# A state-space, attention and feed-forward kernel on one core: the skip term D u moved from TensorE to VectorE in PSUM, and other weights for the steps between the feed-forward's products

## The chip, the cores and the metric

The kernel runs on one core of one Trainium2 chip. The metric is the device time of one execution in microseconds. Five engines work side by side, each through its own queue in order: PE (TensorE, matmuls), DVE (VectorE), ACT (ScalarE), POOL (GpSimd) and SP (SyncE, which issues most of the transfers). Matmul results are written to PSUM, of which the kernel uses eight banks of 128 partitions by 512 fp32 values.

## The reference, cut to what matters

The input is 8 images of 384 channels and 32 x 32 pixels. Two layers follow each other; everything is fp32.

```python
# layer 0, per image, in both directions over L = 1024 pixels
u, z   = split(in_proj(rmsnorm(x)));  u = silu(causal_conv4(u))
dt, B, C = split(x_proj(u));  delta = softplus(dt_proj(dt) + bias)
h[l] = exp(delta * A) * h[l-1] + delta * u * B[l]        # 16 states per channel
y    = sum_n h[l, n] * C[l, n] + u * D_param             # u * D_param is the skip term
g    = out_proj(y * silu(z))                             # forward and backward are added
x    = x + res_scale * (scale_mod * g + sigmoid(dwconv3x3(xn)) * xn)
# layer 1
t = t + attention(layernorm(t))                          # 6 heads, causal over 1024 tokens
h = quant(W1b @ layernorm(t) + b1)                       # scale from max |h| of the whole image
t = t + quant(W2b @ gelu(h) + b2)                        # feed-forward, images 0 to 4 alone here
```

The scale of quant needs the maximum over all of h, so the Gelu and the second product can start only when the first product is complete. Work for other images can be placed in between.

## The kernel before, in words

**Tiles.** Channels lie on the 128 partitions, in three chunks c of 128. The 1024 tokens are cut in two halves h of 512, one PSUM bank each. The images are handled in the order 0, 1, 2, 3, 5, 6, 4, 7.

**Stages.** `before_scan(b)` normalises an image, projects it, does the short convolution, the gates (`gates`, 16 tap multiply-adds of the local convolution on DVE, Silu and Tanh on ACT), the x-projection (`project`) and the step sizes (`delta`). It writes to DRAM what the scan reads. The scan works through 96 units of two states per image. A unit has a multiply on POOL (`s_first`, L588), two exponentials on ACT (L601), two scans on DVE (L606), a second multiply on POOL (L612), and eight transposes with accumulation on PE (`s_sum`, L620), which sum the states in the bank `y`. `attention(b)` does the output projection, the attention and, for images 0 to 4, collects the steps of `feed_forward(b)`.

**The gate.** When a chunk's half is complete in both directions, `s_gate` puts it together, 48 times in all. It loads the half of u (`us`, the sum over both directions) and of silu(z) (`sz`) from DRAM, into one buffer each. It takes a bank of the tag `pt`, which has two. On PE it multiplies u by a diagonal matrix of D (`diagd`, built at the start, L183; the product is L656, two matmul instructions in the trace, as for every fp32 product here) and adds the transposed sums of the scan onto it (L661). DVE multiplies the bank by `sz` (L670) and SP writes the result out. The profile's names are `yb` for the bank, `ush` for the loaded u and `zh` for the loaded silu(z).

**The feed-forward.** It has 24 first-product steps (`hp`, L995), then the scale of h (`quant_scale`: a maximum on DVE, one transposition on PE named `row_h`, L963, and four small DVE operations), then the Gelu step (four ACT instructions over 128 x 3072, L1018, and four DVE minima, L1021, both raised in priority by 60 instructions), then six second-product steps (`yp`, L1039), a second scale (`row_y`) and three output steps. The weights of both products are loaded by SP as they are needed, from a pool of ten buffers (`mid`) that `before_scan` also uses.

**The order.** Each stage emits its work as steps, pairs of a function and an estimated length in us (2.5 if none is given). `spread_over` merges two lists so that both advance at the same share of their own total: a step's place is its middle divided by its list's total. The steps of a feed-forward are merged in this way with those of a later image's `before_scan`, for the first four images of the order (the later images are 5, 6, 4 and 7). The lengths in the merged list are multiplied by `JOINT` = 0.6. The feed-forward of image 4 has nothing left to be merged with. All lists of attention and feed-forward are joined to `rest`, and the scan units are placed evenly between due times that are sums of the lengths in `rest`. The resulting order is an order of priority: the framework's scheduler then makes each engine's queue from it, and may put an instruction that is ready before one that is not. Instructions in `pin` keep their written order.

The lines that do the merging:

```python
        if fed and later:
            fed = spread_over(fed, steps_of(before_scan, later.pop(0), ("pt", "pt", "av")))
            fed = [(f, JOINT * us) for f, us in fed]
        rest += fed
```

Of the kernel before, what the change touches and what calls it, by code (L numbers as in the profile page):

```python
# [12 lines left out]
ALU = mybir.AluOpType  # L13
# [4 lines left out]
P = 128  # L18
B, C, H, W = 8, 384, 32, 32
L = H * W  # L20
NC = C // P
# [18 lines left out]
DW = BC0 + 2 * NS  # L40
PARTS = ((0, 0), (0, 1), (1, 1), (1, 0))
JOINT = 0.6
SET = 8
HURRY = 400
AHEAD = 2
# [4 lines left out]
V_NORM, V_CW, V_CB, V_DTB, V_D, V_DW, V_DWB, V_BP, V_B2, V_ALOG = 0, 1, 5, 6, 7, 8, 17, 18, 19, 20  # L50
# [4 lines left out]
def kernel(  # L55
# [16 lines left out]
    nc = tc.nc  # L72
# [11 lines left out]
    def ctile(name, shape, dt=F32):  # L84
        return const.tile(shape, dt, name=name, tag=name)
# [44 lines left out]
    vec = ctile("vec", [P, NC, NV])  # L130
# [8 lines left out]
    for d in range(2):  # L139
        nc.scalar.dma_start(out=wdt[d * DW : d * DW + RANK, :], in_=w_dt)  # L140
        nc.scalar.dma_start(
            out=wdt[d * DW + RANK : d * DW + RANK + 1, :],
# [13 lines left out]
    ident = ctile("ident", [P, P])  # L156
# [21 lines left out]
    amat = ctile("amat", [P, NC, NS])  # L178
    nc.scalar.activation(amat, vec[:, :, V_ALOG : V_ALOG + NS], AF.Exp)
    nc.vector.tensor_scalar(amat, amat, -1.0, None, ALU.mult)  # L180
    diagd = ctile("diagd", [P, NC, P])
    for c in range(NC):
        nc.vector.tensor_scalar(diagd[:, c, :], ident, vec[:, c, V_D : V_D + 1], None, ALU.mult)  # L183
    rssm = ctile("rssm", [P, 1])
    nc.vector.tensor_tensor(rssm, sc[:, 0:1], sc[:, 1:2], ALU.mult)
    rsh = ctile("rsh", [P, 1])
# [357 lines left out]
    class Unit:  # L544
        def __init__(self, b, part, c, n):
            self.b, self.c, self.part, self.n = b, c, part, n
            self.d, self.h = PARTS[part]
            self.name = f"{b}_{c}_{part}_{n}"
            self.asks = c == (0 if n % (2 * SET) < SET else NC - 1)

# [3 lines left out]
        for part in range(len(PARTS))  # L554
        for k in range(NS // SET)
        for c in (range(NC) if k % 2 == 0 else reversed(range(NC)))
        for n in range(k * SET, (k + 1) * SET, 2)
    ]
# [84 lines left out]
    def s_gate(u):  # L643

        if not u.last:
            return
        b, c, h = u.b, u.c, u.h
        yts = sst.pop(("yt", b, c, h))
        both = []
        for what in ("us", "z"):  # L650
            t = sp.tile([P, HB], F32, name=f"{what}h_{u.name}", tag=what, bufs=1)
            load(t, spilled[b, what, c][:, half(h)])
            both.append(t)
        us, sz = both
        tp = bank(f"yb_{u.name}", "pt")
        nc.tensor.matmul(  # L656
            out=tp, lhsT=diagd[:, c, :], rhs=us, start=True, stop=False, skip_group_check=True
        )
        for yt in yts:
            for i in range(QT):  # L660
                nc.tensor.matmul(  # L661
                    out=tp[:, chunk(i)],
                    lhsT=yt[:, i, :],
                    rhs=ident,
                    is_transpose=True,
                    start=False,
                    stop=(yt is yts[-1] and i == QT - 1),
                    skip_group_check=True,
                )
        nc.vector.tensor_tensor(sz, sz, tp, ALU.mult)  # L670
        t = dram.tile([P, HB], F32, name=f"sgy_{u.name}", tag=f"sp_gy_{c}_{h}")
        nc.sync.dma_start(out=t, in_=sz)
        spilled[b, "gy", c, h] = t
# [296 lines left out]
    def feed_forward(b, t, emit):  # L970
        st = {}

        @emit
        def _():
            st["xn"] = t()
            st["mxh"] = small.tile([P, NF], F32, name=f"mxh_{b}", tag="mxh", bufs=1)
            st["mxy"] = small.tile([P, NC], F32, name=f"mxy_{b}", tag="mxy", bufs=1)

        layernorm(t, f"nf_{b}", emit)
        for m in range(NF):  # L980
            for h in range(NH):

                @emit.of(3.1)
                def _(m=m, h=h):
                    if m % NC == 0 and h == 0:
                        st["h", m // NC] = btile(f"h{m // NC}_{b}")
                    if m % 2 == 0 and h == 0:
                        st["w1"] = mtile(f"w1_{b}_{m}").rearrange("p (c e) -> p c e", c=4)
                        load(
                            st["w1"][:, :NC, :],  # L990
                            w1s[:, m * P : (m + 2) * P].rearrange("(c p) e -> p c e", p=P),
                        )
                    hp = bank(f"hp_{b}_{m}_{h}", "s")
                    for c in range(NC):
                        nc.tensor.matmul(  # L995
                            out=hp,
                            lhsT=st["w1"][:, c, chunk(m % 2)],
                            rhs=st["xn"][:, c, half(h)],
                            start=(c == 0),
                            stop=(c == NC - 1),  # L1000
                        )
                    hm = st["h", m // NC][:, m % NC, :]
                    nc.scalar.activation(hm[:, half(h)], hp, AF.Identity, bias=b1t[:, m : m + 1])
                    if h == NH - 1:
                        nc.vector.tensor_reduce(
                            st["mxh"][:, m : m + 1], hm, AX.X, ALU.max, apply_absolute_value=True
                        )

        @emit.of(3.0)
        def _():  # L1010
            st["s1"] = quant_scale(st["mxh"], f"h_{b}")


        @emit.of(3.0)
        def _():
            with tc.high_priority(offset=60):
                for q in range(NF // NC):
                    pin(nc.scalar.activation(st["h", q], st["h", q], AF.Gelu, scale=st["s1"]))  # L1018
                pin(nc.scalar.preload_act_table_set(LOG_EXP))
                for q in range(NF // NC):  # L1020
                    nc.vector.tensor_scalar(st["h", q], st["h", q], QCLIP, None, ALU.min)  # L1021

        for m in range(NC):
            for h in range(NH):

                @emit.of(10.7)
                def _(m=m, h=h):
                    if m == 0 and h == 0:
                        st["y"] = btile(f"yf_{b}")
                    if h == 0:  # L1030
                        for k in range(0, NF, 6):
                            w = mtile(f"w2_{b}_{m}_{k}", 6 * P).rearrange("p (k e) -> p k e", k=6)
                            load(
                                w, w2s[k * P : (k + 6) * P, chunk(m)].rearrange("(k p) e -> p k e", p=P)
                            )
                            st["w2", k // 6] = w
                    yp = bank(f"yp_{b}_{m}_{h}", "s")
                    for k in range(NF):
                        nc.tensor.matmul(  # L1039
                            out=yp,  # L1040
                            lhsT=st["w2", k // 6][:, k % 6, :],
                            rhs=st["h", k // NC][:, k % NC, half(h)],
                            start=(k == 0),
                            stop=(k == NF - 1),
                        )
                    ym = st["y"][:, m, :]
                    nc.scalar.activation(
                        ym[:, half(h)], yp, AF.Identity, bias=vec[:, m, V_B2 : V_B2 + 1]
                    )
                    if h == NH - 1:  # L1050
                        nc.vector.tensor_reduce(
                            st["mxy"][:, m : m + 1], ym, AX.X, ALU.max, apply_absolute_value=True
                        )

        @emit.of(3.0)
        def _():
            st["s2"] = quant_scale(st["mxy"], f"y_{b}")

        for m in range(NC):

            @emit
            def _(m=m):
                to = mtile(f"t3_{b}_{m}")
                load(to, spilled[b, "t2", m])
                for h in range(NH):
                    ym = bank(f"yq_{b}_{m}_{h}", "s")
                    nc.vector.tensor_scalar(
                        ym, st["y"][:, m, half(h)], st["s2"], QCLIP, ALU.mult, ALU.min
                    )
                    th = to[:, half(h)]  # L1070
                    nc.vector.scalar_tensor_tensor(th, ym, -QCLIP, th, ALU.max, ALU.add)
                nc.sync.dma_start(out=out[b, chunk(m), :], in_=to)


    class Steps(list):
# [4 lines left out]

        def of(self, us):
            return lambda f: self(f, us)

    def spread_over(*lists):

# [64 lines left out]
    for i, b in enumerate(ORDER):  # L1150
        if i > 0:
            due.append((sum(us for _, us in rest), i * per))
        fed = Steps()
        rest += steps_of(attention, b, fed) if i < B - 1 else []
        if fed and later:
            fed = spread_over(fed, steps_of(before_scan, later.pop(0), ("pt", "pt", "av")))
            fed = [(f, JOINT * us) for f, us in fed]
        rest += fed

    timed, here = [], 0  # L1160
# [63 lines left out]
```

## Time and profile before

| what | value |
|---|---|
| median of 3 runs | 4989.93 us (4987.43 to 4991.37) |
| the profiled execution's own time | 4984.05 us |
| its span, first to last instruction | 4982.3 us |
| granted TensorE clock, mean | 0.884 of full speed |
| instructions | 50788 |

The profile is of one execution. In it, the images' attention parts begin about 832, 1482, 2160, 2837, 3530, 3880, 4239 and 4773 us after the span's start. Images 5 and 6 have no feed-forward, so that their rounds take some 350 us in place of some 680. The gap between the last first-product matmul and the first second-product matmul was:

| image | last hp ends, us | Gelu, us | first yp starts, us | gap, us |
|---|---|---|---|---|
| 0 | 1319.5 | 1340.3 to 1351.4 | 1355.7 | 36.2 |
| 1 | 1992.0 | 2009.2 to 2020.4 | 2036.8 | 44.8 |
| 2 | 2676.0 | 2698.9 to 2710.0 | 2714.3 | 38.4 |
| 3 | 3357.0 | 3379.6 to 3390.7 | 3400.9 | 43.9 |
| 4 | 4667.1 | 4679.7 to 4690.8 | 4686.1 | 18.9 |

Profile lines are read as follows. A group is a source line, engine, operation and the tiles it writes and reads, with how often it ran; then its busy time in us, the mean of one in ns, and how long the engine was idle just before it, with what ended that idle time. PEld is the loading of a matmul's stationary operand and runs beside PE. SPq is SP's queue of transfers.

### The profile page before, as it was taken

The numbers are of one execution on the slowest core, as the hardware profiler recorded it, in microseconds if no ns is written. First come the engines' busy times: TensorE is split into PE (matmuls) and PEld (weight loads), VectorE is DVE, ScalarE is ACT, GpSimd is POOL, SyncE is SP. The second block draws the span as 40 slices with busy tenths as digits, with TensorE's granted clock in tenths as the row PEclk, the third lists the DMA queues.
The fourth block names the chain that finished last, engine by engine and source line by source line (L and its number), as shares of the span: only waits on it lengthen the run. The fifth ranks groups of instructions, "written<-read, shape, count | busy, mean of one in ns | idle before, by whom it ended". The sixth has DMA issues, their size and how long they took to land. (4 is left out here: it accounts for less than half of the span.)

```text
span 4982.3 us, 50788 instructions
## 1 busy us (share of the span) xinstructions
PE 4058.8 (81%) x16458; PEld 2192.3 (44%) x16458; DVE 3607.8 (72%) x4771; ACT 2668.1 (54%) x4858; POOL 3696.0 (74%) x1944
## 2 busy tenths in 40 slices
PE   3687786988888888788787888887888988888989
PEld 1243343544444444345443444443454544444444
DVE  6887988677886768786778867687867676676623
ACT  4575655565554655545656446555456365464425
POOL 0578687997768986779876788867789888888800
PEclk7788797899989899888998888998899988999999
DMA  6554646324463335463334633334533333334210
GB/s 230 204 185 151 200 164 229 114 93 130 140 220 120 112 116 168 136 200 123 100 125 147 210 111 129 112 130 157 193 130 116 113 110 124 131 102 137 93 58 26
DMA packets 365010, 696.36 MB, mean 140 GB/s; under 512 B 30104, under 2 KB 88904, under 8 KB 364744
## 3 DMA queue, kind: packets, MB, share of 16 engines
q1 hardware_dynamic: 355232, 676.97, 40.9%
q10 hardware_dynamic: 9512, 16.15, 0.9%
q8 instruction: 130, 2.13, 0.2%
q14 instruction: 136, 1.11, 0.1%
HBM read 527.33 MB, written 165.68 MB: 139 GB/s over the span
## 5 line engine op out<-in xcount | busy, mean ns | idle before, releaser
L588 POOL TENSOR_TENSOR g<-ud,bc 128x1024 f32<-128x1024 f32 x768 | 1840.4, 2396 | 579.8 <-PE y L620 452.0
L612 POOL TENSOR_TENSOR g<-g,bc 128x1024 f32<-128x1024 f32 x768 | 1822.1, 2373 | 251.7 <-DVE g L606 157.8
L601 ACT ACTIVATE da<-dl,amat 128x512 f32<-128x512 f32 x1536 | 1057.3, 691 | 1532.5 <-DVE g L606 1498.3
L606 DVE TENSOR_TENSOR_SCAN g<-da,g 128x512 f32<-128x512 f32 x768 | 906.5, 1210 | 475.4 <-POOL g L588 457.2
L606 DVE TENSOR_TENSOR_SCAN g<-da,carry,g 128x512 f32<-128x512 f32 x768 | 953.3, 1271 | 384.2 <-POOL g L588 354.1
L620 PE MATMUL y<-ident,g 128*128 128x128 f32 x6144 | 949.1, 303 | 266.7 <-POOL g L612 123.1
L620 PEld LDWEIGHTS y<-ident,g 128*128 128x128 f32 x6144 | 789.3, 156 | 714.4 <-issue 418.9
L788 PE MATMUL s<-k,q 64*128 64x512 f32 (+3 forms) x1152 | 384.5, 600 | 128.9 <-DVE nm L802 110.5
L802 DVE CUSTOM_DVE_ANT_0 pr<-s,cmask 128x512 f32<-128x512 f32 (+3 forms) x576 | 299.5, 545 | 178.2 <-PE s L788 177.9
L812 ACT ACTIVATE pr<-pr,nm 128x512 f32<-128x512 f32 (+3 forms) x576 | 348.9, 607 | 123.5 <-DVE nm L802 121.6
L864 PE MATMUL pt<-ident,pr 128*128 128x128 f32 x1728 | 304.0, 309 | 93.6 <-ACT ptn L866 55.1
L995 PE MATMUL hp<-t,w 128*128 128x512 f32 x720 | 334.9, 610 | 28.7 <-DMA w<-w1s 18.3
L1039 PE MATMUL yp<-h,w 128*128 128x512 f32 x720 | 332.6, 620 | 15.3 <-DMA w<-w2s 12.1
L864 PEld LDWEIGHTS pt<-ident,pr 128*128 128x128 f32 x1728 | 217.7, 155 | 245.0 <-ACT ptn L866 110.3
L877 PE MATMUL av<-ptn,v 128*64 128x512 f32 (+3 forms) x1152 | 273.1, 555 | 50.4 <-ACT ptn L866 33.9
L341 PE MATMUL in<-xn,win 128*128 128x512 f32 x576 | 282.3, 636 | 32.3 <-DVE xc L463 8.6
L866 ACT COPY ptn<-pt 128x512 f32<-128x512 f32 (+3 forms) x576 | 255.3, 472 | 49.8 <-PE pt L864 48.4
L727 PE MATMUL qp<-t,wqk 128*128 128x512 f32 x576 | 266.4, 613 | 11.7 <-DVE t L302 9.1
L400 DVE SCALAR_TENSOR_TENSOR loc<-xn,vec,loc 128x496 f32<-128x496 f32 (+3 forms) x384 | 259.9, 721 | 19.5 <-ACT loc L389 18.2
L788 PEld LDWEIGHTS s<-k,q 64*128 64x128 f32 x1152 | 132.3, 206 | 261.2 <-DVE nm L802 179.6
L611 POOL COPY carry<-g 128x2 f32<-128x2 f32 x384 | 87.0, 226 | 205.9 <-DVE g L606 205.8
L1039 PEld LDWEIGHTS yp<-h,w 128*128 128x128 f32 x720 | 142.0, 201 | 189.1 <-issue 169.4
(153 smaller groups left out, 4722.4 us busy)
## 6 DMA issues: line engine op xcount, KB each, us to landing
bc<-rows SPq DMA_DIRECT2D x512, 512.0 KB, 4.1
dl<-sdl SPq DMA_DIRECT2D x160, 256.0 KB, 2.9
ud<-sud SPq DMA_DIRECT2D x160, 256.0 KB, 2.7
t<-st SPq DMA_DIRECT2D x63, 512.0 KB, 5.1
su<-u SPq DMA_DIRECT2D x48, 512.0 KB, 3.4
du<-su SPq DMA_DIRECT2D x96, 256.0 KB, 3.8
sdl<-du SPq DMA_DIRECT2D x96, 256.0 KB, 2.8
sud<-du SPq DMA_DIRECT2D x96, 256.0 KB, 2.3
```

Of the source, the lines that this page charges most:

```text
L341: nc.tensor.matmul(out=mp, lhsT=st["win", c][:, k, i, :], rhs=st["xn"][:, k, half(h)], start=(k == 0), stop=(k == NC - 1),)
L588: pin(nc.gpsimd.tensor_tensor(g, ud, sst["bc", 0, u.b, u.part, u.n], ALU.mult))
L601: nc.scalar.activation(da, sst["dl", u.b, u.c, u.part], AF.Exp, scale=amat[:, u.c, n : n + 1])
L606: nc.vector.tensor_tensor_scan(gi[:, ::step], da[:, ::step], gi[:, ::step], first, ALU.mult, ALU.add)
L612: pin(nc.gpsimd.tensor_tensor(g, g, sst["bc", 1, u.b, u.part, u.n], ALU.mult))
L620: nc.tensor.matmul(out=y[:, j, :], lhsT=g[:, i, chunk(j)], rhs=ident, is_transpose=True, start=(u.opens and i == 0 and j == 0), stop=(u.cl ...
L788: mm = nc.tensor.matmul(out=ss[e][:, : k1 - k0], lhsT=st["q"][rows_of(e), c, chunk(qi)], rhs=st["k"][rows_of(e), c, k0:k1], start=True, st ...
L802: nc.vector.tensor_tensor_reduce(out=x, in0=ss[e][:, :w], in1=mask, scale=-1.0, scalar=-MASKED, op0=ALU.add, op1=ALU.min, accum_out=m,)
L812: nc.scalar.activation(x, x, AF.Exp, bias=m, scale=-1.0, accum_out=rs[:, i, e, kb : kb + 1])
L864: nc.tensor.transpose(pt[:, chunk(i)], pr[:, e, chunk(j % QT)], ident)
L995: nc.tensor.matmul(out=hp, lhsT=st["w1"][:, c, chunk(m % 2)], rhs=st["xn"][:, c, half(h)], start=(c == 0), stop=(c == NC - 1),)
L1039: nc.tensor.matmul(out=yp, lhsT=st["w2", k // 6][:, k % 6, :], rhs=st["h", k // NC][:, k % NC, half(h)], start=(k == 0), stop=(k == NF - 1),)
```

## The change

The diagonal matrices of D and the product with them are removed. The first transposition into the bank now starts its accumulation. After the last one DVE computes `us * D + tp` in place in PSUM, and the multiplication by silu(z) follows as before.

In the feed-forward, the steps of the two scales and of the Gelu get lengths of 9, 16 and 9 us in place of 3 each, as a `Gap`. A `Gap` is a float that can be told apart. Its length counts when the feed-forward's steps are merged with a later image's; afterwards it is set back to `SHORT` = 3.0. That reset stands in the merging branch, so for the feed-forward of image 4 the long lengths go into `rest`.

```diff
+SHORT = 3.0
...
-    diagd = ctile("diagd", [P, NC, P])
-    for c in range(NC):
-        nc.vector.tensor_scalar(diagd[:, c, :], ident, vec[:, c, V_D : V_D + 1], None, ALU.mult)
...
         tp = bank(f"yb_{u.name}", "pt")
-        nc.tensor.matmul(
-            out=tp, lhsT=diagd[:, c, :], rhs=us, start=True, stop=False, skip_group_check=True
-        )
         for yt in yts:
             for i in range(QT):
                 nc.tensor.matmul(
...
                     is_transpose=True,
-                    start=False,
+                    start=(yt is yts[0] and i == 0),
                     stop=(yt is yts[-1] and i == QT - 1),
                     skip_group_check=True,
                 )
+        nc.vector.scalar_tensor_tensor(tp, us, vec[:, c, V_D : V_D + 1], tp, ALU.mult, ALU.add)
         nc.vector.tensor_tensor(sz, sz, tp, ALU.mult)
...
-        @emit.of(3.0)
+        @emit.of(Gap(9.0))
         def _():
             st["s1"] = quant_scale(st["mxh"], f"h_{b}")
...
-        @emit.of(3.0)
+        @emit.of(Gap(16.0))
         def _():
             with tc.high_priority(offset=60):
                 for q in range(NF // NC):
...
-        @emit.of(3.0)
+        @emit.of(Gap(9.0))
         def _():
             st["s2"] = quant_scale(st["mxy"], f"y_{b}")
...
+    class Gap(float):
+        pass
...
             fed = spread_over(fed, steps_of(before_scan, later.pop(0), ("pt", "pt", "av")))
-            fed = [(f, JOINT * us) for f, us in fed]
+            fed = [(f, JOINT * (SHORT if isinstance(us, Gap) else us)) for f, us in fed]
```

## The prediction

> **What bounds the kernel now.** I read the busy shares and slices of the page first, then the groups by line and shape, then busy time by stage, then PE's timeline in one gap between the two products of the feed-forward, and last who waits for the gate's product.
>
> The busy shares of the page, and its row of granted clocks:
> ```profile
> PE 4058.8 (81%) x16458; PEld 2192.3 (44%) x16458; DVE 3607.8 (72%) x4771; ACT 2668.1 (54%) x4858; POOL 3696.0 (74%) x1944
> PEclk7788797899989899888998888998899988999999
> ```
> No engine is full. PE is nearest to it, and the rows below show why the others are not far.
>
> Busy time by stage (window, its length, then per engine busy us and instructions; then clock, DMA share, GB/s). The rows are, for the second batch in the order, attention, first product, the gap, second product, tail; the last row is the gap of the feed-forward that has no later batch beside it:
> ```profile
> 1482.00:1842.00 360.00, 302.80 (x1402) 171.73 (x1402) 250.64 (x368) 187.73 (x397) 308.47 (x160) 0.88 0.38 126
> 1879.00:1992.00 113.00, 100.91 (x347) 51.20 (x348) 90.49 (x106) 62.88 (x92) 72.76 (x43) 0.95 0.52 170
> 1992.00:2037.00 45.00, 17.43 (x72) 10.08 (x72) 33.55 (x37) 32.87 (x36) 39.07 (x23) 0.75 0.22 65
> 2037.00:2136.00 99.00, 88.49 (x256) 43.32 (x257) 74.47 (x78) 47.94 (x73) 62.55 (x31) 0.89 0.58 187
> 2136.00:2160.00 24.00, 20.43 (x68) 12.88 (x67) 23.76 (x28) 14.18 (x24) 18.32 (x7) 0.60 0.67 223
> 4667.00:4686.00 19.00, 11.36 (x70) 8.80 (x68) 13.63 (x15) 12.33 (x11) 19.00 (x9) 0.82 0.17 47
> ```
> Attention: PE 84%, POOL 86%. The two products: PE about 90%. The gap: PE 39% in 45 us. The tail: DVE 99%. The last gap: POOL 100%. So the bound changes by stage, and PE's time is worth most in the products, least in the gap and the tail.
>
> PE in that gap:
> ```profile
> 1991.82 2.74 PE L341 MATMUL in<-xn,win 128*128 128x512 f32 x6
> 1994.39 1.04 PE L620 MATMUL y<-ident,g 128*128 128x128 f32 x8
> 2008.06 0.44 PE L963 MATMUL row_h<-ident,col_h 128*128 128x128 f32 x1 [12.63 <-DVE col_h L961]
> 2018.26 2.78 PE L620 MATMUL y<-ident,g 128*128 128x128 f32 x24
> 2036.83 3.75 PE L1039 MATMUL yp<-h,w 128*128 128x512 f32 x4 [12.12 <-DMA w<-w2s]
> ```
> Two waits make it: for the maximum of h (row_h), and here for a weight load, elsewhere for ACT, which is in the Gelu. The 24 transposes there are three scan units where the written order has one: instructions that are ready are already drawn forward into the gap.
>
> The groups that the skip term touches, and who waits for the gate's last reader of the bank:
> ```profile
> L656 PE MATMUL yb<-ush,diagd 128*128 128x512 f32 x96 | 60.0, 712 | 3.7 <-ACT ptn L866 1.8 <-DVE du L527 1.1 <-ACT u L379 0.5
> L369 DVE SCALAR_TENSOR_TENSOR u<-up,vec,u 128x512 f32<-128x512 f32 x90 | 66.0, 745 | 3.4 <-ACT u L358 3.3
> L670 DVE TENSOR_TENSOR zh<-zh,yb 128x512 f32<-128x512 f32 x48 | 32.0, 667 | 22.3 <-PE yb L661 22.3
>   PEld pt L864: 27.0, 12
>   PE pt L864: 22.5, 11
> ```
> The reader is to see that L369 is the added instruction's form exactly: PSUM in place plus one SBUF tensor and a column.
>
> **The Trainium skill.** "SBUF — State Buffer", Who interferes with whom: a DVE instruction with at most one SBUF input does not contend with GpSimd, one with two does. The trace agrees: L369 stays at 722 to 757 ns, while L528 with two SBUF inputs has a median of 683 and goes up to 2856 ns (mean 1193). So 0.745 us holds beside POOL. "PSUM — Partial Sum Buffer", The four PSUM rules: the first matmul's start flag clears the bank, and later ones overwrite columns not yet written. So the start on the first transpose can replace the diagonal product; no row here times it. "TensorE: Matmul & The Clock Gate", Part 1: an idle window of some 3.4 us halves PE's clock. The trace agrees in kind: 0.75 in the gap, 0.95 in the first product. PE work in a half-idle gap is dear in its own time, cheap in the kernel's.
>
> **The change, part by part.** The sum is against the profiled execution, 4984.05 us (span 4982.3 and 1.75 around it). The median of the runs shown is 5.9 us above.
>
> *Diagonal product out.* 48 gates, each two matmuls. From the first one's start to the next instruction's start PE spends 1.30 us on the mean of the 48 (712 ns is one matmul's modelled time): 62.4 us. Not all counts. Six gates lie before 832 us, where DVE is busy 688 of 832 us and PE 568: no credit. After about 14 others PE waits for L670 (the list above), so an earlier arrival only waits longer. That leaves 28 gates, 36.4 us. PE is busy in 84% of 832 to 4757 us (3287 of 3925); I credit that share: -30.5 us. Bounds: 0, and -62.
>
> *Three diagonals at the start out* (0.28 us each on DVE): 0.8 us ahead of the first scan, while the first weights are still being loaded; counted as nothing, -0.8 if that stage hangs on DVE.
>
> *Product on DVE in.* 48 x 0.745 = 35.8 us. The six in the first stage count in full, 4.5. The other 42 make 31.3 us; DVE idles 28% of that stretch, mostly for POOL (811 us over the run), which is the cover. Where it is missing, scans, score masks and the maxima queue behind. I count a fifth, 6.3. Together +10.8; bounds +4.5 and +35.8.
>
> *Bank and buffer held longer.* The bank comes free one DVE instruction later. Where PE waits for it (14 times) that is 14 x 0.745 = 10.4 us; two thirds count, as PE is two to five us late for other reasons at some: +7. The us buffer, of which there is one, is released by DVE and no longer by PE, some 3 us later (the median from the last transpose to L670); its next load, on SP, has 20 us to the next gate, and nothing waits on ush in the views. Counted 0, bounds 0 and +5. No semaphore is added that another engine must meet sooner; DVE itself now waits for ush, which its zh load, issued together, already made it do.
>
> First edit: -30.5 + 10.8 + 7 = -13.
>
> *Gap weights in the four joint feed-forwards.* From the code's costs: the feed-forward's list grows from 181.6 to 206.6 and the later batch's is 180.2. Its steps between the last first-product step and the first second-product step go from 12.8 to 27.8 units. By name: before, the set-up of the third chunk and four input projections; now also the second chunk's two x-projections and one conv half. The gates step of that chunk moves to just ahead of the last first-product step, from about four steps earlier, and one input projection leaves its place ahead of row_h for one behind it. Planner costs are reset to 3.0 here, so scan slots stay. Real work moved: two x-projections, 4 matmuls of 0.54 us on PE, 2.2 us, and two adds of 0.67 on DVE; a conv half, two ACT of 0.69 and three DVE of 0.745. PE idles 15.6 to 27.5 us in these gaps, so 2.2 us goes there free. Against it, row_h loses 2.7 us of cover. The second product's weight loads stay on SP behind the same scan loads; the third chunk's tiles are asked for at the same place. I take -2 each, -8; bounds +10 each (the rival below) and -8 each (the sparser products gain all they lose). The second quantization's weight moves one more delta into the tail, 3.9 us of DVE by its four rows; it also leaves a stretch where DVE is 75% busy: within the bounds.
>
> *The lone fifth feed-forward.* Its weights are not reset, so the plan of the last stretch grows from 488 to 513 while it holds 96 units: by the code's arithmetic four units fewer stand ahead of the last first-product step, and six instead of two before the second product. PE saves 4 x 0.87 = 3.5 us earlier. In the gap POOL is already full, and a unit costs it 4.77 us (2396 ns of L588 and 2373 of L612): 19 us if all is waited for, less the 7.7 us that PE idles there now: +12. Some of those transposes are drawn forward already, so +6; bounds -3.5 and +12.
>
> Sum: -13 - 8 + 6 = -15: 4969 on the profiled execution, 4975 as a median.
>
> **Rivals.** *PE is the bound everywhere* (products at 90%, POOL waiting 452 us for L620): 62 saved, 6 paid to DVE, 5 in each gap: -76, 4914. Against: 14 waits behind the bank. *Hidden anyway*: the gap is already filled by what is ready, and DVE pays back what PE gains: 0, 4990. For it: the 24 transposes above. *The second product starts later*, slower: the chunk's gates, 16 multiply-adds of 0.72 and more, some 16 us of DVE, now stand just ahead of the maximum of h, while row_h already waits 7.8 to 12.8 us. If half of it delays row_h, 8 + 2.7 us a gap, 43 for four; with +12 in the fifth and -13 of the first edit, +42: 5032; with half that delay, +20, 5010. It decides once the gaps (36, 45, 38, 44 us) grow by about 2 us each. Against: much of those gaps is already ACT's and the weight load's. That the change does less than it says is part of the second rival: only 2.2 us of PE work is moved per gap.
>
> **How the numbers follow.** Forecast 0.42, own range 4955 to 4985. PE everywhere 0.11, hidden 0.20, later start 0.27. A difference under 0.2%, 10 us, is what a measurement of this kernel can't tell from none. The forecast is mostly beyond it on the fast side (0.38 faster, 0.04 same); with the first rival 0.49 faster. Same: 0.04 + 0.18 of the hidden case, 0.22. Slower: 0.27 and the rest of the hidden case, 0.29. The range, 4925 to 5022, takes in the bounds up to the middle of both outer rivals.
>
> **What would show it.** Right: L656 gone, 48 instructions of about 0.745 us in its place; PE's busy time some 60 us lower, its stretch between 832 and 4757 shorter by 10 to 20 us; gaps within 3 us of before with about 2 us more PE work; the last gap longer by 6 to 12. Wrong: row_h waiting 15 us or more and gaps over 47 us (later start); PE's idle time grown by as much as its work fell (hidden); L864 waiting over 80 us for zh (the bank).

## The result, and the profile after

The changed kernel is faster by 0.6%. Its time as a ratio to the kernel before is 0.994, with a 95% interval of 0.9927 to 0.9952: about 30 us less, between 24 and 36. The forecast was 15 us less. So the direction was right and the size half of what was measured.

| | before | after |
|---|---|---|
| median, us | 4988.61 (12 runs) | 4954.81 (12 runs) |
| the profiled execution, us | 4984.05 | 4954.67 |
| its span, us | 4982.3 | 4952.9 |

Busy time of the engines and the row of granted clocks, from the page of the changed kernel:

```profile
PE 4026.1 (81%) x16362; PEld 2178.9 (44%) x16362; DVE 3641.0 (74%) x4820; ACT 2681.3 (54%) x4864; POOL 3687.0 (74%) x1944
PEclk7787796999889899888898888898888989989899
```

PE lost 32.7 us of busy time, DVE gained 33.2. The shares have hardly moved: still no engine is full.

The groups at the gate, by line and shape, in the changed kernel:

```profile
L656 PE MATMUL yb<-ident,yt 128*128 128x128 f32 x384 | 62.4, 309 | 7.3 <-ACT ptn L862 2.3 <-DVE t L701 1.9 <-ACT z L346 1.5
...
L665 DVE SCALAR_TENSOR_TENSOR yb<-ush,vec,yb 128x512 f32<-128x512 f32 x48 | 35.8, 745 | 28.5 <-PE yb L656 18.3 <-issue 7.5 <-ACT da L599 2.8
...
L666 DVE TENSOR_TENSOR zh<-zh,yb 128x512 f32<-128x512 f32 x48 | 32.2, 671 | 0.1
```

The diagonal product is gone (L656 is now the line of the transposes). The added instruction takes 745 ns, the very mean of L369 from which it was priced. The wait for the transposes moved with the first reader of the bank, from the multiplication by silu(z) to L665. Who waited for this bank's last reader, from the view of the tile `yb` of the changed kernel (us, times):

```profile
  PE pt L860: 7.7, 11
...
  PEld pt L860: 5.8, 8
```

Before, the same two rows had 22.5 and 27.0 us. The two rows mostly count the same waits, once for the matmul and once for its weight load; counted once, they cover 27.1 us before and 10.0 after. The forecast expected this wait to grow. How it could shrink is taken up in the experiments.

Busy time by stage, for the second image again (attention, first product, gap, second product, tail), and for the gap of image 4:

```profile
1480.00:1836.00 356.00, 289.04 (x1404) 164.22 (x1405) 257.30 (x375) 188.66 (x401) 311.44 (x162) 0.91 0.39 127
1880.00:1975.00 95.00, 89.35 (x292) 44.62 (x290) 79.96 (x92) 56.00 (x82) 59.56 (x35) 0.99 0.50 176
1975.00:2016.00 41.00, 22.70 (x81) 12.48 (x81) 32.73 (x33) 28.78 (x30) 29.54 (x18) 0.74 0.23 71
2016.00:2108.00 92.00, 85.46 (x261) 43.12 (x261) 78.13 (x81) 48.62 (x73) 72.31 (x38) 0.93 0.60 195
2108.00:2139.00 31.00, 19.33 (x67) 11.51 (x64) 30.66 (x35) 16.97 (x31) 18.52 (x7) 0.65 0.65 227
...
4625.00:4657.00 32.00, 14.84 (x83) 13.03 (x82) 27.20 (x19) 19.72 (x15) 32.00 (x12) 0.63 0.32 107
```

For this image, attention is 4 us shorter with 14 us less work on PE. The gap has more on PE (22.7 for 17.4 us) and is 4 us shorter, and the tail is 7 us longer. The last gap is 32 us in place of 19, with POOL full in both.

PE in the gap of image 1, changed kernel, in order of time (start, duration; in brackets the idle time before and who ended it):

```profile
1972.54 2.74 PE L991 MATMUL hp<-t,w 128*128 128x512 f32 x6
...
1978.47 1.97 PE L618 MATMUL y<-ident,g 128*128 128x128 f32 x8 [3.20 <-POOL g L610]
1980.37 3.68 PE L485 MATMUL xp<-u,wx 128*64 128x512 f32 x8
1984.62 0.27 PE L959 MATMUL row_h<-ident,col_h 128*128 128x128 f32 x1
1985.16 3.60 PE L339 MATMUL in<-xn,win 128*128 128x512 f32 x8
...
2009.80 1.97 PE L618 MATMUL y<-ident,g 128*128 128x128 f32 x8 [10.71 <-POOL g L610]
2016.42 3.75 PE L1035 MATMUL yp<-h,w 128*128 128x512 f32 x6
```

The x-projections have come in, as the forecast's arithmetic of the code said. But `row_h`, which waited 12.6 us for the maximum, no longer waits. Over the five feed-forwards PE's matmuls waited 43.3 us for it before, and 0.7 us now.

**By stage.** Each cell is worked out from the marks in the traces (start of an attention, start of the feed-forward's normalisation, which ends it, last first-product matmul, first second-product matmul, end) as the difference to the kernel before, in us. "Four rounds" are images 0 to 3, "two rounds" are images 5 and 6, which have no feed-forward. First product is taken with the gap behind it, second product with the tail.

| kernel | attention, four rounds | first product and gap | second product and tail | two rounds | gap of image 4 | rest | sum |
|---|---|---|---|---|---|---|---|
| before, us | 1429.4 | 766.3 | 502.3 | 708.5 | 18.9 | | |
| after | -12.7 | -23.7 | -0.5 | -0.9 | +12.7 | -4.3 | -29.4 |
| a_skip_on_dve | -25.9 | +3.3 | +0.1 | -14.7 | 0.0 | -5.1 | -42.2 |
| b_gap_weights | +13.9 | -33.2 | -3.4 | +5.4 | +15.3 | +0.4 | -1.6 |
| c_reset_last | -15.4 | -20.8 | -4.2 | -1.9 | +9.3 | -5.8 | -38.9 |
| d_first_gap_reset | -22.7 | -16.2 | +3.1 | -5.5 | 0.0 | -2.7 | -44.0 |
| e_no_skip | -26.3 | +3.7 | +1.0 | -8.8 | 0.0 | -1.0 | -31.4 |
| f_both | -6.5 | +10.4 | +3.1 | +3.2 | +9.2 | +7.9 | +27.3 |
| l_off_bank | +4.5 | -0.1 | -2.1 | 0.0 | +9.3 | +6.3 | +17.9 |
| g_scale_first | -27.7 | +7.0 | +1.9 | -10.1 | 0.0 | -5.7 | -34.5 |
| h_wider | -39.8 | -9.8 | -1.9 | -10.5 | 0.0 | -5.4 | -67.3 |
| v_3_37 | -23.2 | -32.4 | +8.0 | -12.5 | +9.3 | -6.0 | -56.7 |
| v_37_3 | -37.1 | -22.0 | +5.6 | -7.7 | 0.0 | -3.9 | -65.1 |
| j_widest | -29.3 | +13.2 | +2.6 | -8.5 | +9.2 | -5.7 | -18.4 |

It is read with care: each row is one execution, and one execution lies up to 22 us from the median of its own kernel (a_skip_on_dve 4942 against 4963, v_3_37 4927 against 4906). Places are read from the table, with the same caution; sizes from the timed runs.

### The profile page after: what moved, and what is told of

The parts are those of the page before. It is cut to its first block, busy times and chain, and to the rows that moved or that the text cites. A ratio compares the mean times of both kernels' runs of the same rounds, so it can differ in the third digit from the quotient of the medians.

```text
span 4952.9 us, 50623 instructions
## 1 busy us (share of the span) xinstructions
PE 4026.1 (81%) x16362; PEld 2178.9 (44%) x16362; DVE 3641.0 (74%) x4820; ACT 2681.3 (54%) x4864; POOL 3687.0 (74%) x1944
## 5 line engine op out<-in xcount | busy, mean ns | idle before, releaser
L991 PE MATMUL hp<-t,w 128*128 128x512 f32 x720 | 336.8, 614 | 31.7 <-DMA w<-w1s 15.4
L991 PEld LDWEIGHTS hp<-t,w 128*128 128x128 f32 x720 | 135.3, 196 | 191.0 <-issue 145.9
```

What stands on the lines that cost most here:

```text
L991: nc.tensor.matmul(out=hp, lhsT=st["w1"][:, c, chunk(m % 2)], rhs=st["xn"][:, c, half(h)], start=(c == 0), stop=(c == NC - 1),)
```

## The experiments

Each kernel is timed against the kernel before on the same chip; ratios have 95% intervals.

| kernel | what it is | ratio | interval | median, us |
|---|---|---|---|---|
| a_skip_on_dve | first edit alone | 0.994 | 0.9917 to 0.9963 | 4963.2 |
| b_gap_weights | second edit alone | 0.9973 | 0.9963 to 0.9983 | 4976.9 |
| c_reset_last | after, lengths reset for image 4 too | 0.992 | 0.9898 to 0.9942 | 4947.7 |
| d_first_gap_reset | c, second scale back at 3 | 0.9917 | 0.9896 to 0.9938 | 4948.8 |
| e_no_skip | before, without the skip term | 0.994 | 0.9928 to 0.9952 | 4952.6 |
| f_both | before, plus a DVE pass on the bank | 1.0041 | 1.0028 to 1.0055 | 5004.3 |
| l_off_bank | before, plus a DVE pass off the bank | 1.0007 | 0.9996 to 1.0017 | 4987.7 |
| g_scale_first | a, scale of h at higher priority | 0.994 | 0.9926 to 0.9954 | 4950.9 |
| h_wider | d with lengths 14 and 26 | 0.9886 | 0.987 to 0.9902 | 4925.6 |
| v_3_37 | d with lengths 3 and 37 | 0.9863 | 0.9843 to 0.9884 | 4905.6 |
| v_37_3 | d with lengths 37 and 3 | 0.9883 | 0.9865 to 0.9901 | 4919.3 |
| j_widest | d with lengths 20 and 40 | 0.9939 | 0.9922 to 0.9956 | 4950.8 |

**The two edits apart.** a_skip_on_dve is the changed kernel with its `Gap` lengths at 3:

```diff
-        @emit.of(Gap(9.0))
+        @emit.of(3.0)
...
-        @emit.of(Gap(16.0))
+        @emit.of(3.0)
...
-        @emit.of(Gap(9.0))
+        @emit.of(3.0)
```

> The first edit alone: the skip term on DVE, all weights 3.0 as before. Theory P (the sum of the prediction: PE's freed time counts in part, DVE and the bank take some back): -13 us, ratio 0.997. Theory E (PE is the bound wherever a gate lies): -35 to -56 us, ratio 0.989 to 0.993, which would be all of the measured gain and more. Theory G (the gain is the gap's weights): 0 to -5 us, ratio 0.999 to 1.000. The fifth gap should be back near 19 us in all three.

b_gap_weights is the kernel before with those lengths and the reset, the product on PE kept:

```diff
-        @emit.of(3.0)
+        @emit.of(Gap(9.0))
...
-        @emit.of(3.0)
+        @emit.of(Gap(16.0))
...
-        @emit.of(3.0)
+        @emit.of(Gap(9.0))
...
-            fed = [(f, JOINT * us) for f, us in fed]
+            fed = [(f, JOINT * (SHORT if isinstance(us, Gap) else us)) for f, us in fed]
```

> The second edit alone: the weights of 9, 16 and 9, the diagonal product still on PE. Theory P: -8 in the joint feed-forwards and +6 in the fifth, so -2 us, ratio 1.000, and a fifth gap of some 25 to 32 us. Theory E: 0 to +8, as the gain is PE's product. Theory G: -25 to -30 us, ratio 0.994 to 0.995, in spite of a longer fifth gap.

Each edit gains by itself: about 30 us (18 to 41) and 13.5 us (8 to 18). The forecast had given them 13 and 2. Neither ratio is that of one theory: a_skip_on_dve lies between P's 0.997 and E's 0.989 to 0.993, b_gap_weights between P's 1.000 and G's 0.994 to 0.995. They gain in different places. The table puts all of a_skip_on_dve into attention and the two rounds without feed-forward, where the scans run densest. It does the same for e_no_skip and g_scale_first. It puts the gain of b_gap_weights, 33 us, into the first product and the gap, but in that execution attention and the gap of image 4 take 29 us back. In the waits of POOL, the row for PE's transposed sums has changed (line waited for: us in total, times, longest). The kernel before:

```profile
POOL g L588 <- PE y L620: 452.0, 202, 14.1
```

a_skip_on_dve:

```profile
POOL g L586 <- PE y L618: 380.1, 178, 15.0
```

POOL, which feeds every scan, waits 72 us less for PE to free its buffers. The row doesn't tell the two edits apart: in b_gap_weights it is 403.3 us, 49 less than before. Together the edits gain about 30, not 43; with the intervals above that shortfall can't be told from none.

**The last feed-forward and the second scale.** c_reset_last takes image 4's lengths back; d_first_gap_reset also returns the second scale to 3:

```diff
-        rest += fed
+        rest += [(f, SHORT if isinstance(us, Gap) else us) for f, us in fed]
```

> The changed kernel with the long lengths set back to 3.0 for image 4 too. If the fifth gap's 12.8 us of growth are its price, and what it takes from the stages before is small: -8 to -12 us against the changed kernel, ratio to before 0.991 to 0.992, the fifth gap near 19 us. If the units that stood there are only moved: within 4 us of the changed kernel, ratio 0.993 to 0.995.

> As the run before, with the weight of the second quantization at 3.0, so that no further delta step moves into the tail of the joint feed-forwards. If the delta in the tail, where DVE is full, costs its 3.9 us each: -8 to -16 us against the run before, most of it between the last second-product matmul and the next image's output projection. If the second product gains as much as the tail loses: within 4 us of the run before.

PE in the gap of image 4 in the changed kernel:

```profile
4636.60 1.97 PE L618 MATMUL y<-ident,g 128*128 128x128 f32 x8 [1.64 <-POOL g L610]
4641.24 1.97 PE L618 MATMUL y<-ident,g 128*128 128x128 f32 x8 [2.67 <-POOL g L610]
4647.40 1.97 PE L618 MATMUL y<-ident,g 128*128 128x128 f32 x8 [3.76 <-POOL g L610]
4655.03 1.97 PE L618 MATMUL y<-ident,g 128*128 128x128 f32 x8 [5.24 <-POOL g L610]
4656.80 3.62 PE L1035 MATMUL yp<-h,w 128*128 128x512 f32 x4
```

The second product stands behind four more scan units on PE's queue, each of which waits for POOL. That is the mechanism of the forecast, at 12.7 us, just over its upper bound of 12. In d_first_gap_reset the gap is back at 18.9 us. The timed runs put c_reset_last 0.2% and d_first_gap_reset 0.23% ahead of the changed kernel, with overlapping intervals: the sign fits, the size is not resolved. Between c and d there is nothing to be told apart, so the second scale's length is worth nothing that shows here.

c_reset_last did not get its 12.7 us back in its profiled execution: its gap stayed 9.3 us longer, for a reason that isn't the order of the steps (last section). If its timed runs have that too, it blurs the comparison of c with the changed kernel and with d.

**What the DVE instruction costs.** e_no_skip leaves the skip term u * D out altogether:

```diff
-        nc.tensor.matmul(
-            out=tp, lhsT=diagd[:, c, :], rhs=us, start=True, stop=False, skip_group_check=True
-        )
...
-                    start=False,
+                    start=(yt is yts[0] and i == 0),
```

> The kernel before without the skip term at all: neither the diagonal product on PE nor its replacement on DVE (it leaves u * D_param out of y). It prices PE's freed time alone. The first edit alone gave 0.994 (about -29 us). Theory P, with the credit mis-sized: DVE and the bank cost the 18 us that the prediction charged, so PE's time is worth 47: ratio 0.990 to 0.991. Theory H (PE's time is worth the 30.5 predicted and the DVE work is hidden behind its waits for POOL): ratio 0.993 to 0.995, no better than the first edit alone.

f_both keeps the product on PE and adds a DVE pass over the bank of the same kind, which adds 0 times u:

```diff
+        nc.vector.scalar_tensor_tensor(tp, us, 0.0, tp, ALU.mult, ALU.add)
         nc.vector.tensor_tensor(sz, sz, tp, ALU.mult)
```

> The kernel before with the diagonal product on PE kept and one DVE instruction more per gate, of the added form, which adds zero times u to the bank. It prices the DVE work and the bank's longer hold alone. Theory P: +18 us, ratio 1.0035. Theory H: -2 to +5 us, ratio 0.9995 to 1.001. If PE's and DVE's shares add up, this ratio times that of the run without the skip term gives 0.994.

l_off_bank spends about the same DVE time on `us` alone, after the bank's last reader (the multiplication by silu(z)), on a result that nobody reads:

```diff
         nc.vector.tensor_tensor(sz, sz, tp, ALU.mult)
+        idle = small.tile([P, 1], F32, name=f"idle_{u.name}", tag="col")
+        nc.vector.tensor_reduce(idle, us, AX.X, ALU.max)
```

> The kernel before, diagonal product kept, with one DVE instruction more per gate that doesn't touch the bank: a maximum over the 512 values of us, placed after the multiplication by silu(z), its result unused. The instruction on the bank cost 1.0041 (+20 us). If DVE's own time is the price: nearly the same, ratio 1.002 to 1.004. If the longer hold of the bank and the later result are: ratio 0.999 to 1.001. Its 0.6 us is a little shorter than the 0.67 us on the bank.

Without the term the kernel gains 0.6% (24 to 36 us of 4981); with the term on DVE it gains 0.6% as well (a_skip_on_dve, and g_scale_first on the same chip as e_no_skip, which turned out to be the same kernel as far as its time goes). Between g_scale_first and e_no_skip the two intervals leave some 9 us either way for the price of the 48 DVE instructions. The forecast had charged 10.8 for DVE time and 7 for the bank.

The price is not nothing wherever the instruction stands. The DVE groups of the two additions, f_both by line and shape:

```profile
L670 DVE SCALAR_TENSOR_TENSOR yb<-ush,yb 128x512 f32<-128x512 f32 x48 | 32.6, 680 | 26.8 <-PE yb L661 26.7
```

and l_off_bank, from the view of its tile `idle` (durations: least, median, most):

```profile
L672 DVE TENSOR_REDUCE idle<-ush x48: 655/678/689, 218.1 to 4776.8; 128x1 f32<-128x512 f32 x48
```

Both take 0.68 us 48 times, some 32.6 us of DVE. On the bank behind the product it costs about 20 us (14 to 27); off the bank about 3 (-2 to +8), not to be told from nothing. So DVE time as such was covered, and what is dear in f_both is the instruction's place between the transposes and the gate's result. The 20 us may hold something else besides: of the 27 us more in f_both's profiled execution, 9.2 are in the gap of image 4 (last section). l_off_bank has 9.3 there too, so the comparison of these two stands.

In the change the same place costs nothing that can be measured. So the parts don't add up: 0.994 without the term times 1.0041 for the added pass is 0.998, and the first edit alone measured 0.994. The time that a gate holds its bank, from the first PE instruction into it to the end of the multiplication by silu(z), has these medians over the 48 gates: before 5.68 us, a_skip_on_dve 5.93, f_both 7.32, e_no_skip 3.81, worked out from the traces. The product's own PE time left the hold as DVE's instruction entered it, and DVE came to the bank sooner after the last transpose, 1.13 us against 2.99. So against the kernel before the hold hardly grew. But the hold is not the price by itself: a_skip_on_dve holds the bank 2.1 us longer than e_no_skip and is not measurably slower, while the kernel before holds it no longer than a_skip_on_dve and takes some 30 us more. Why the instruction is dear behind the product and free in its place is open.

By which instruction f_both pays its 20 us isn't settled. PE's waits for the bank's last reader, each counted once, are no longer in it than before (24.4 us against 27.1), so it isn't simply the next user of the bank. POOL's wait for PE's sums is 469 us in it, 452 before, 401 in e_no_skip and 380 in a_skip_on_dve, much the same direction as the times. But the row doesn't rank the kernels: it is 416 us in v_3_37, the fastest, and 451 in l_off_bank. That it is the cause is not shown.

**Why row_h came earlier.** g_scale_first asked whether a maximum of h that comes earlier is worth time by itself, on the kernel of the first edit alone:

```diff
-            st["s1"] = quant_scale(st["mxh"], f"h_{b}")
+            with tc.high_priority(offset=60):
+                st["s1"] = quant_scale(st["mxh"], f"h_{b}")
```

> The first edit with weights of 3.0, and in place of the gap weights the scale of h raised in priority by 60 instructions, as the Gelu is. It brings row_h forward and moves no step of the later image. If the gap weights gain because the scale stands ahead of the scan unit and the input projection: the wait from the last first-product matmul to row_h falls by 3 to 10 us a gap, and the ratio is about that of the changed kernel with the reset, 0.991 to 0.993. If they gain because work leaves the two products for the gap: about that of the first edit alone, 0.994, although row_h is earlier.

It failed as a test of either theory: the time from the last first-product matmul to `row_h` stayed as it was (1.7 us less over four gaps, as in a_skip_on_dve), because what was late stood ahead of the scale. ACT's timeline shows it. The kernel before, around the end of the first product (1992.0 us):

```profile
1991.57 0.67 ACT L1003 ACTIVATE h<-hp,b1t 128x512 f32<-128x512 f32 x1
...
1995.81 0.69 ACT L601 ACTIVATE da<-dl,amat 128x512 f32<-128x512 f32 x1 [2.99 <-DVE g L606]
...
2000.67 0.69 ACT L601 ACTIVATE da<-dl,amat 128x512 f32<-128x512 f32 x1 [2.46 <-DVE g L606]
...
2002.41 0.67 ACT L1003 ACTIVATE h<-hp,b1t 128x512 f32<-128x512 f32 x1
```

The changed kernel, around the same end (1975.3 us):

```profile
1974.22 1.28 ACT L455 ACT_TABLE_LOAD   x1
1975.52 1.30 ACT L599 ACTIVATE da<-dl,amat 128x512 f32<-128x512 f32 x2
1976.76 0.67 ACT L999 ACTIVATE h<-hp,b1t 128x512 f32<-128x512 f32 x1
```

Before, the last eviction of h sat in ACT's queue behind exponentials of the scan, which wait for DVE's scans; after the end of the product 3, 5, 2 and 4 of them still ran ahead of it in the four gaps. After the change it was 0, 2, 0 and 0. From the last first-product matmul to `row_h` the four gaps together took 54.9 us before and 29.6 after. Why the scheduler's order came out so isn't shown.

The earlier `row_h` did not shorten the gaps, which took 163.3 us together before and 168.0 after. What got shorter is the first product ahead of them (from the feed-forward's normalisation on): 603.0 us before and 574.6 after over the four images, with 31 us less DVE work in it (492.6 to 461.6) and 20 us less on PE (524.1 to 504.4).

The last four kernels vary how much of the later image's work goes into the gap, and where in it, all on d_first_gap_reset (first length before the Gelu step, second at it):

```diff
-        @emit.of(Gap(9.0))
+        @emit.of(Gap(14.0))
...
-        @emit.of(Gap(16.0))
+        @emit.of(Gap(26.0))
```

h_wider, 14 and 26:

> As the run with the first gap alone and the reset, with weights of 14 and 26 in place of 9 and 16. The gates step (16 multiply-adds on DVE and more) and all four conv halves of the third chunk then stand in the gap. If work that leaves the products is what gains: -5 to -15 us against the run with 9 and 16, ratio 0.989 to 0.991. If the gap's chain is DVE's by then: row_h later by up to 8 us a gap, gaps of 50 us and more, and no gain or a loss, ratio 0.992 to 0.996.

v_3_37, 3 and 37:

> As the run with 14 and 26, the same 40 in all, but 3 for the scale and 37 for the Gelu: the scale stands ahead of the second chunk's gates, and all that moves stands between it and the second product. If the Gelu's wait is what the moved work fills: as good as 14 and 26 or better, 0.987 to 0.989. If the wait ahead of row_h is: worse, 0.991 to 0.993.

v_37_3, 37 and 3:

> The same 40 turned round, 37 for the scale and 3 for the Gelu: gates, x-projections, all input projections and two conv halves stand between the last first-product step and the Gelu. If the wait ahead of row_h is what the moved work fills: 0.987 to 0.989. If the chain to the Gelu is pushed back by DVE's and ACT's added work: gaps 10 us longer than with 14 and 26, ratio 0.992 to 0.995.

j_widest, 20 and 40:

> As the run with 14 and 26, with 20 and 40. One conv half of the second chunk comes into the gap besides. If there is still idle time to fill: 0.985 to 0.988. If the gap is full: longer gaps and no gain over 14 and 26, 0.988 to 0.992.

The amount counts: 25 units in all give 0.9917, 40 give 0.9863 to 0.9886, 60 give 0.9939. Every kernel with 40 is clear of the one with 60; only v_3_37 is clear of 25 on its interval. Where the 40 stand makes no difference that the intervals can tell: v_3_37 has the gain expected if the Gelu's wait is filled, and v_37_3 the gain expected if the wait ahead of `row_h` is, so neither wait is singled out. j_widest is slower than both its theories said, no better than the first edit alone (0.994). v_3_37 is the best of all kernels run, 1.4% below the kernel before (1.2 to 1.6), and its interval is clear of the changed kernel's. Busy time by stage for image 1, first product and gap, in v_3_37:

```profile
1839.00:1981.00 142.00, 128.01 (x429) 66.54 (x428) 114.96 (x137) 88.37 (x131) 104.68 (x55) 0.94 0.46 151
1981.00:2022.00 41.00, 24.11 (x97) 14.00 (x96) 36.50 (x40) 32.87 (x34) 25.27 (x15) 0.80 0.26 84
```

The first product over the same stretch in the kernel before:

```profile
1842.00:1992.00 150.00, 132.32 (x466) 68.09 (x465) 122.98 (x145) 87.66 (x134) 105.87 (x57) 0.97 0.47 151
```

The first product is 8 us shorter, with 8.0 us less on DVE and 4.3 less on PE. This gap is not longer than before (45 us) and has DVE busy 89% of it in place of 75%. In j_widest the same gap:

```profile
1982.00:2038.00 56.00, 28.78 (x114) 17.45 (x112) 48.81 (x52) 36.82 (x40) 39.57 (x21) 0.72 0.27 90
```

It holds 49 us of DVE work in 56 us. In all four images, worked out from the traces of one execution each:

| kernel | first product, us | DVE busy in it, us | four gaps, us | DVE busy in a gap |
|---|---|---|---|---|
| before | 603.0 | 492.6 | 163.3 | 66 to 76% |
| after | 574.6 | 461.6 | 168.0 | 78 to 90% |
| h_wider | 551.3 | 451.1 | 205.2 | 83 to 92% |
| v_3_37 | 559.3 | 453.5 | 174.6 | 87 to 91% |
| v_37_3 | 555.1 | 450.9 | 189.2 | 83 to 95% |
| j_widest | 566.0 | 443.1 | 213.5 | 85 to 93% |

In the kernel before, POOL is the fullest engine of the four gaps (84 to 91% busy); in the others it is DVE. From 40 units to 60 the gaps grow while the product no longer shrinks. That DVE sets this limit is argued, not shown. A longer gap alone is no sign of loss: h_wider has gaps of 47.6, 61.4, 51.0 and 45.3 us and gains. And the product with its gap is not all of it. In h_wider and v_37_3 the table by stage puts 14 to 17 us more of the gain into attention than in d_first_gap_reset, and little or none into the product and its gap. Why is open.

## Why the prediction was right, and where its sizes failed

- *The product out of PE, -30.5 us.* Right in size: e_no_skip measures -30 (-24 to -36). Its working isn't confirmed. The credit was spread evenly from 832 to 4757 us, and the gain lay in some stages only (next but one), so that the sum comes out so closely is partly luck. e_no_skip also frees the bank sooner.
- *The product onto DVE, +10.8, and the bank held longer, +7.* The step of the first edit that failed. Together they came to nothing that can be measured, within some 9 us. Two parts of it were wrong. The bank was hardly held longer than before, as the product's PE time had been part of the hold: 5.93 us for 5.68. And PE's waits for it fell, 27.1 us to 10.8, where the term had them grow by the instruction's length 14 times. Of the DVE time, the six gates of the first stage were charged in full, 4.5 us, but that stage is 0.8 us shorter in a_skip_on_dve. The rest was covered; l_off_bank shows the same for as much DVE time, though behind the gate's result. That the price is nothing only once the product is gone, f_both shows; why, stays open.
- *Where the gain of PE would lie.* It was credited evenly over the stretch from 832 to 4757 us. It lies in the attention stages and the two rounds without feed-forward, in a_skip_on_dve as in e_no_skip and g_scale_first.
- *PE's busy time some 60 us lower.* It fell by 33. The product's row lost its 60.0. The transposes into the same bank took 6.9 us more (290 to 309 ns each), and other rows in sum some 20 more; the busy time of PE is only loosely tied to the work removed. The stretch from 832 to 4757 us, forecast 10 to 20 us shorter, is 28 us shorter.
- *Gap weights, -2 a gap.* The right sign, mis-sized. The whole second edit was put at -2 (-8 + 6) and measured -13.5 alone. The step that failed is "real work moved": it priced the moved work by the 2.2 us of PE that go into the gap free, and named the DVE and ACT instructions without pricing them. The first product is nearly as full on DVE (123 of 150 us) as on PE, and it lost 31 us of DVE work over the four images as it got 28 us shorter. That the one caused the other is argued, not shown.
- *Row_h loses 2.7 us of cover*, and the rival in which it comes later still. Wrong: it came earlier, by 25 us over four gaps. Both looked at what stands behind and ahead of it on PE and DVE; what it waited for was the last eviction in ACT's queue.
- *Gaps within 3 us of before.* Over the four together, +4.7. One by one no: 43.3, 41.1, 45.5 and 38.1 us against 36.2, 44.8, 38.4 and 43.9. What stands ahead of the gap in one plan and in it in the other differs, so the product and its gap have to be read as one.
- *The last feed-forward, +6 (bounds -3.5 to +12).* The mechanism as described; the gap grew by 12.7 us, where the working gave 19 less 7.7, that is 11.4, and then took half off for transposes drawn forward. What it costs the kernel is not resolved by c_reset_last and d_first_gap_reset.
- *PE the bound everywhere*, 4914, fails: POOL's waits for PE fell by 80 us, and the time by 30. *Hidden anyway*, 4990, fails on the interval.

The two errors in the sum, 18 us charged at the gate and 11 us too little for the gap weights, add up to more than the 15 us missing; the rest is what the two edits don't gain together, which the intervals don't resolve.

## What to carry to other kernels

When an accumulated term moves from one engine to another, the time of the added instruction is not its price, and the price is not the same in every place. Here an instruction of some 0.7 us, run 48 times, cost about 20 us behind the old product, about 3 us off the bank (not told from nothing), and nothing measurable in the product's stead. Time the removal, the addition and the whole, since they need not add up. When work is moved into a gap, price it by every engine that is nearly full where it leaves, judge the stage and its gap together, and try several amounts: here 40 units were best, and 60 were no better than no long lengths at all. A reduction's wait at the head of a gap can be set by the last eviction in an in-order queue, as on ACT here, so look at what stands ahead of that before moving the reduction.

## What the runs showed of the hardware that was not expected

The four DVE minima after the Gelu (128 x 3072, in SBUF) take 1.75 us each when alone, and much longer beside POOL, in two ways. d_first_gap_reset, the timeline of the gap of image 4, DVE's line and then POOL's:

```profile
4637.39 14.91 DVE L1017 TENSOR_SCALAR h<-h 128x3072 f32<-128x3072 f32 x4 [0.38 <-ACT h L1014]
...
4639.12 3.92 POOL L610 TENSOR_TENSOR g<-g,bc 128x1024 f32<-128x1024 f32 x1
4642.98 3.88 POOL L586 TENSOR_TENSOR g<-ud,bc 128x1024 f32<-128x1024 f32 x1
```

c_reset_last, the same place:

```profile
4633.64 17.65 DVE L1017 TENSOR_SCALAR h<-h 128x3072 f32<-128x3072 f32 x4 [0.37 <-ACT h L1014]
...
4635.40 2.33 POOL L610 TENSOR_TENSOR g<-g,bc 128x1024 f32<-128x1024 f32 x1
4637.70 2.35 POOL L586 TENSOR_TENSOR g<-ud,bc 128x1024 f32<-128x1024 f32 x1
4640.02 2.34 POOL L610 TENSOR_TENSOR g<-g,bc 128x1024 f32<-128x1024 f32 x1
...
4646.34 18.97 PE L1035 MATMUL yp<-h,w 128*128 128x512 f32 x37 [11.64 <-DVE h L1017]
```

In the first the two engines take turns: a POOL multiply goes from 2.36 to 3.9 us. In the second the first of the minima takes 12.6 us, while five POOL multiplies pass at full speed, and the second product waits for it: the gap is 9.3 us longer. The other three take 1.75 us each, with no POOL multiply beside them. Which of the two happens differs between kernels with the same order of steps there; f_both and l_off_bank, whose order is that of the kernel before, have gaps longer by the same 9.2 and 9.3 us, and so have v_3_37 and j_widest. It is not new with the change either: one minimum of image 2 takes 8.75 us in the kernel before. The Trainium skill ("SBUF — State Buffer", Who interferes with whom) says that a DVE instruction in a two-port mode and GpSimd lock each other out, the first to issue holding the pair for the whole instruction. That the minima run in such a mode is not shown here. The first case agrees with it. In the second, several POOL instructions went by within the time of one DVE instruction, so that its wait, if that is what it was, isn't bounded by the one POOL instruction that issued first.
